# A retention and FFN sandwich on one core: one more tile of x1n by way of VectorE and DRAM, input combinations on VectorE, and a new order at the seam between blocks

## The chip, the cores and the metric

The kernel runs on one core of one Trainium2 chip. The metric is the device time of one execution in microseconds (us), the median of several executions. All engine times below come from one profiled execution.

## The reference

The input x has 4 sequences of 1024 tokens with 512 features, all in f32. With LN a layernorm without weights:

```python
x = x + LN(attn(LN(x)));   x = x + LN(ffn(LN(x)))

attn(x):  q, v, g = x @ Wq.T, x @ Wv.T, silu(x @ Wg.T)       # 512 x 512 each
          ret[t] = lam[head] * ret[t-1] + v[t]                # a scan along the sequence
          return (LN(q * ret) * gamma + beta) * g @ Wo.T
ffn(x):   gate, up = silu(x @ f8(gate_w) * gate_s), x @ f8(up_w) * up_s    # 512 -> 1536
          return gate * up @ f8(down_w) * down_s                           # 1536 -> 512
```

f8() rounds a weight to 8-bit float.

## The kernel before

The 4096 tokens are cut into 8 **blocks** of 512 tokens, each of 4 **tiles** of 128 tokens (s = 0 to 3). The main loop (line 1048) goes over stages t = 0 to 7. Stage t computes the FFN of block t (object `f`), and between its matmuls it slips in the attention of block t+1 (object `b`) and the preparation of block t+2 (object `n`). Inside a stage, i = 0 to 11 goes over the 12 groups of 128 hidden features of the FFN. Every engine works through its instructions in the order in which this loop issues them (`InOrder`, line 66): there is no scheduler that reorders. All instructions have line 74 in the profile, so they are told apart by the names of tiles.

**The FFN of one i.** TensorE multiplies into two PSUM tiles, `pfg` (gate) and `pfu` (up), 8 matmuls each: 4 chunks of features, each with an upper and a lower half of the f32 value of x1n. ScalarE applies silu to `pfg`; VectorE multiplies it with `pfu` (the line `gate<-pfu`); ScalarE casts the product to the upper half `fuse` (`fuse`), and VectorE computes the lower half (`rest`, the line `fuse<-gate,fuse`). Two iterations later TensorE multiplies that by the down weights into `pd`, 8 matmuls. `pfg` and `pfu` take turns in two PSUM buffers (tag `pf`).

**The attention in products.** From block 2 on (`FAST`), each of the four 512x512 projections is computed as 7 products of halves, with sums and differences of halves of the weights and of the data, instead of 8 products. One product is 4 f32 matmuls of 256 columns, recorded as 8. The products are numbered j = 1 to 7 and are made in the order of the list `order` (line 333); `product` (line 481) makes the next one, asks SP for the weights of a later one (`fetch_weights`, a ring of 4 buffers) and lets VectorE or ScalarE take the result out of PSUM. Written v1, v2 and so on for the projection v, what comes after a product is:

- v1: ScalarE copies it to SBUF. v2 adds to the same bank, and VectorE then runs two scans on it.
- v6: in the other bank; VectorE adds the copy of v1 (`mids<-pv`). v7 adds to that bank, again with one VectorE addition; v4, v5 and v3 follow.

The right side of v1 and v2 is a half of the normalized and transposed input `xnT`. The others need a combination of halves in `t_sums`, made by `input_sums` (line 465): combination 1 and then 2 (which reads 1) for v6, 3 for v7, 4 (which reads 2) for v4. One combination is one 128x512 subtraction.

**The seam between stages.** The FFN of block t+1 can start its first `pfg` when x1n of that block is there, transposed and in two halves (`x1nT`), for all four tiles. Per tile the steps are these:

- `o_moments(s)`: mean and variance of the attention's output on VectorE (`st<-mids`, `mv<-st`), and its power -1/2 on GpSimd. The `mv` tiles have 3 buffers.
- `x1_of(s)`: ScalarE normalizes it, GpSimd adds it to x, and SP stores the sum x1 to DRAM (`kept`).
- `x1_moments(s)`, `x1n_of(s)`: the same moments for x1, and VectorE normalizes it (`x1n<-x,mv`).
- The transposition. Tiles 0 and 1 go by `move_x1n` (line 754): VectorE transposes blocks of 32x32 (`xs<-x1n`), SP stores them to DRAM in four pieces (`mxs<-xs`), and a load brings them back in order (`x1n<-mxs`). Tiles 2 and 3 go by `turn_x1n` (line 751): 4 transposes on TensorE into a `pf` tile (`pt`).
- `upper_of(s)`: ScalarE casts the upper half into `x1nT`; `rest_of(s)`: VectorE computes the lower half.

In stages 1 to 5 the instructions of TensorE at the seam are: pfg and pfu of i = 11, v1, pd of i = 9, the transposes of tiles 2 and 3, v2, v6, then pfg of the next stage's i = 0, v7, pfu, v4 and so on. GpSimd makes combinations 1 and 2 at i = 9 and 3 and 4 at i = 11. On VectorE the moments of the output tiles 2 and 3 follow the normalization of tiles 0 and 1; `rest(10)` is issued after `x1n_of(3)` in i = 11; the four `rest_of` come before the scans of v2. Stage 6 has the same seam without `n`: no products and no combinations, with tiles 2 and 3 on TensorE before the change and after it.

Of the kernel before, what the change touches and what calls it, by code (L numbers as in the profile page):

```python
# [23 lines left out]
def retention_ffn_sandwich(  # L24
# [26 lines left out]
    NB = NT // TB  # L51
# [14 lines left out]
    class InOrder:  # L66
# [9 lines left out]
    pe, dve, act, pool, sp = (  # L76
        InOrder(e) for e in (nc.tensor, nc.vector, nc.scalar, nc.gpsimd, nc.sync)
    )
# [138 lines left out]
    def rounds(n, now=True):  # L217
        for _ in range(n):
            next(rounding, None)
            if now:  # L220
                units()
# [75 lines left out]
    def ps_tile(name, home="pa"):  # L297
        if home == "pa":
            pa_turn[0] = 1 - pa_turn[0]
            home = f"pa{pa_turn[0]}"  # L300
        elif home[:2] == "pa":
            pa_turn[0] = int(home[2])
        return homes[home].tile([P, TB], F32, tag=home, name=name)
# [26 lines left out]

    FAST = 2
    H = TB // 2
    order = [("v", j) for j in (1, 2, 6, 7, 4, 5, 3)]
    order += [("q", j) for j in (1, 6, 2, 7, 4, 5, 3)]
    order += [("g", j) for j in (1, 2, 6, 7, 4, 5, 3)]
    order += [("o", j) for j in (1, 2, 6, 5, 3, 7, 4)]
    banks = {
        "v": {1: 0, 6: 1, 5: 0}, "q": {1: 1, 6: 0, 5: 1},
        "g": {1: 0, 6: 0, 5: 1}, "o": {1: 0, 6: 1, 5: 0},
# [38 lines left out]
            sp.dma_start(operands[k][j], t)  # L378

    RING = 4  # L380
    total_products = len(order) * (NB - FAST)
    fetched = [0]

    def fetch_weights():
        n = fetched[0]
        if n < total_products:
            k, j = order[n % len(order)]
            sp.dma_start(w_ring[:, n % RING], operands[k][j])
            fetched[0] += 1

    class Retention:
# [88 lines left out]

        def product(self):

            k, j = order[self.made]
            n = (self.t - FAST) * len(order) + self.made
            self.made += 1
            w = w_ring[:, n % RING]
            if j in (1, 6, 5):
                bank = ps_tile(f"p{k}{j}_{self.t}", f"pa{banks[k][j]}").rearrange("p (c f) -> p c f", c=2)
                if j == 6:
                    self.bank_b = bank  # L490
                else:
                    self.bank_a = bank
            bank = self.bank_b if j in (6, 7, 4) else self.bank_a
            for o in range(2):
                out_ = bank[:, o]
                if k != "o" and len(self.right[j].shape) == 4:
                    out_ = out_.rearrange("p (g j) -> p g j", j=Q)
                for c in range(2):
                    if k == "o":
                        left, right = self.left[j][:, c, ts(o, P)], w[:, c, :]  # L500
                    else:
                        left, right = w[:, c, ts(o, P)], self.right[j][:, c]
                    pe.matmul(
                        out_, left, right,
                        start=(j in (1, 6, 5) and o == 0 and c == 0), stop=True,
                        skip_group_check=True,
                    )
            fetch_weights()
            if k == "o":
                return self.add_o(j, bank)  # L510
            c12, p1, s167 = (mids[:, m] for m in (1, 2, 3))
            if k == "v" and self.t == FAST:

                if j == 1:
                    self.p1 = work.tile([P, 2, H], F32, tag="rstd", name="p1", bufs=1)
                p1 = self.p1
            if j == 1:
                act.copy(p1, bank)
            elif j == 6:
                dve.tensor_tensor(c12, bank, p1, ALU.add)  # L520
            elif j == 7:
                dve.tensor_tensor(s167, bank, p1, ALU.add)
            elif j == 2:
                self.take(k, 0, 0, bank)
            elif j == 4:
                dve.tensor_tensor(p1, bank, p1, ALU.add)
                self.take(k, 1, 0, p1)
            elif j == 5:
                dve.tensor_tensor(s167, bank, s167, ALU.add)
                self.take(k, 1, 1, s167)  # L530
            else:
                dve.tensor_tensor(c12, bank, c12, ALU.add)
                self.take(k, 0, 1, c12)
# [195 lines left out]
        def x1_of(self, s):  # L729
            self.x1n[s] = work.tile([P, D], F32, tag="tok", name=f"x1n_{self.t}_{s}", bufs=4)  # L730
            center = shift_scale if self.fast else self.center
            center(self.x1n[s], self.po.pop(s), self.mvo[s])
            pool.tensor_tensor(self.xt[s], self.xt[s], self.x1n[s], ALU.add)
            self.kept[s] = dram.tile([P, D], F32, tag="kept", name=f"kept_{self.t}_{s}")
            sp.dma_start(self.kept[s], self.xt[s])

# [178 lines left out]
    a = Retention(0, x_first)  # L915
# [20 lines left out]
    b = Retention(1)  # L936
# [63 lines left out]
    a.o_moments(0)  # L1000
    rounds(1)
    a.x1_of(0)
    a.o(1, "pd1")
    a.o_moments(1)
    a.x1_moments(0)
    a.x1_of(1)
    a.x1n_of(0)
    a.o(2, "pd2")
    a.o_moments(2)
    a.x1_moments(1)  # L1010
    a.x1_of(2)
    a.x1n_of(1)
    a.o(3, "pd3")
    a.new_x1nT()
# [2 lines left out]
    a.o_moments(3)  # L1017
    a.x1_moments(2)
    a.x1_of(3)
    a.x1n_of(2)  # L1020
    a.rest_of(0)
    b.q(0, "pf")
# [25 lines left out]
    for t in range(NB):  # L1048
        f, n = Ffn(a), None
        fast = b is not None and b.fast  # L1050
        for i in range(NI):
            if t > 0 and (t > 1 or i) and not (fast and i == 11):
                (f if i else l).rest((i - 1) % NI)
            if t == 0 and i == 0:
                n = Retention(2)
# [36 lines left out]
            for _ in range(look[i][0] if t == 1 else 0):  # L1092
                next(search)

            if fast and i < 10:
                b.product()
            if t == 2 and i == 0:
                next(passing)
# [44 lines left out]
            if fast and i == 7:  # L1143
                b.y_sums(3, 4)
            if fast and i == 9:
                b.x1_moments(0)
                b.x1_moments(1)
            if fast and i == 10:
                b.x1_of(2)
                b.x1_of(3)  # L1150
            units()
            f.up(i)
            if n and i == 11:
# [3 lines left out]
            if t == 0 and i == 10:  # L1157
                load = b.move_x1n(2)
# [2 lines left out]
                load()  # L1161
                keep_sums("g")
                b.o_moments(3)
            if b and i == 11:
                b.x1n_of(3, center_scale)
            if fast and i == 11:
                f.rest(10)
            if n and i == 11:
                n.input_sums(*((3, 4) if fast else (1, 2)))
            if t == 0 and i == 11:  # L1170
                b.upper_of(2)
            if fast and i == 9:
                loads = []
                for s in range(2):
                    b.x1n_of(s)
                    loads.append(b.move_x1n(s))
                for load in loads:
                    load()
                if n:
                    n.input_sums(1, 2)  # L1180
            if fast and i == 11:
                for s in range(2):
                    b.upper_of(s)
                    b.rest_of(s)
# [32 lines left out]
            if fast and i == 8:  # L1217
# [1 line left out]
                b.o_moments(1)  # L1219
                b.x1_of(0)  # L1220
                b.x1_of(1)
            if fast and i == 9:
                b.o_moments(2)
                b.o_moments(3)
            if fast and i == 10:
                b.x1_moments(2)
                b.x1_moments(3)
                b.x1n_of(2)
            if t == 0:
                if i == 3:  # L1230
                    rounds(2, now=False)
                    b.halves()
                    units()
                    rounds(1, now=False)
                elif i < 8:
                    rounds(3, now=False)
                if i == 2:
                    b.halves()
                if i < 11:
                    f.rest(i)  # L1240
                if i < 2:
                    n.stats(i)
# [7 lines left out]
                n.new_xnT()  # L1250
            if b and not fast and 7 <= i <= 10:
                b.x1_of(i - 7)
            if b and not fast and i >= 9:
                b.rest_of(i - 9)
            if n and t > 0 and i in (6, 7):
# [32 lines left out]
            if n and i == 11:  # L1288
                if t == 0:
                    n.product()  # L1290
                else:
                    b.turn_x1n(2, "pf")
                    b.upper_of(2)
                    b.rest_of(2)
                b.turn_x1n(3, "pf")
                b.upper_of(3)
                b.rest_of(3)
                if t == 0:
                    n.input_sums(3, engine=dve)
            if fast and (i < 3 or i in (7, 8)):  # L1300
                b.product()
            if fast and i == 2:
# [6 lines left out]
                b.var()  # L1309
                b.rstd_y()  # L1310
            if n and i == 11:
                n.products(2 if t else 1)
                if t == 0:
                    n.input_sums(4, engine=dve)
                    f.rest(11)
# [9 lines left out]
            if b and i == 4 and 0 < t < NB - 2:  # L1325
                n = Retention(t + 2)
# [4 lines left out]
        l, a, b = f, b, n  # L1331
# [68 lines left out]
```

## Time and profile before

| what | value |
|---|---|
| time, median of 3 runs (lowest, highest) | 971.76 us (971.65, 972.81) |
| time of the profiled execution | 971.97 us |
| its span, first to last instruction | 970.2 us |
| granted clock of TensorE, mean | 0.997 |
| busy: PE, weight loads (PEld), VectorE (DVE), ScalarE (ACT), GpSimd (POOL) | 955.9, 764.3, 678.5, 405.9, 282.8 us |
| first weight load of the transposes at the seams after stages 1 to 6 | 310.45, 427.14, 543.50, 659.72, 775.90, 891.47 us |

PE is TensorE's matmuls and PEld its weight loads; a matmul and its weight load are one step of the same queue. A timeline's row gives the start, the time until the end of the group, the engine, the operation with its output and inputs, and the number of instructions put together; what stands in brackets is the time in which the engine was idle before it, and what ended that. A new instruction can start a little before the one before it has ended, so the spacing of starts is often some 0.08 us shorter than a duration.

### The profile page before, as it was taken

How to read it: one execution, taken by the hardware profiler on the slowest of the kernel's cores; microseconds unless marked ns; L12 is line 12 of the kernel's file. 1: busy time of each engine (PE TensorE's matmuls, PEld its weight loads, DVE VectorE, ACT ScalarE, POOL GpSimd, SP SyncE). 2: the span in 40 equal slices, each digit the busy share in tenths (PEclk: the TensorE clock that was granted, in tenths of full speed). 3: DMA queues.
4: the chain of work that ended last, by engine and by line, in shares of the span. 5: the costliest groups of instructions: out<-in, count | busy, mean ns of one | idle time of the engine just before them, and what ended most of it. 6: DMA issues, size and time to landing. Idle time of an engine off the chain costs nothing.

```text
span 970.2 us, 11799 instructions
## 1 busy us (share of the span) xinstructions
PE 955.9 (99%) x4118; PEld 764.3 (79%) x4118; DVE 678.5 (70%) x1038; ACT 405.9 (42%) x637; POOL 282.8 (29%) x356
## 2 busy tenths in 40 slices
PE   9999999999999999999999999999999999999996
PEld 7455766778888888888888888888888888888885
DVE  5996999676767578586685766767667676657535
ACT  3555674468655135331433315342162421524223
POOL 1404131412327042250523315242142602314020
PEclk9999999999999999999999999999999999999998
DMA  9311423762436426463336524364242632314021
GB/s 297 127 48 61 152 66 97 226 209 87 141 98 181 123 89 215 131 183 100 96 111 177 159 76 133 97 175 140 81 153 92 179 116 85 100 44 131 0 87 44
DMA packets 96060, 119.04 MB, mean 123 GB/s; under 512 B 8320, under 2 KB 58240, under 8 KB 96000
## 3 DMA queue, kind: packets, MB, share of 16 engines
q1 hardware_dynamic: 95136, 117.62, 40.0%
q8 instruction: 33, 0.54, 0.2%
q10 hardware_dynamic: 864, 0.66, 0.2%
q14 instruction: 27, 0.22, 0.1%
HBM read 86.00 MB, written 32.24 MB: 122 GB/s over the span
## 4 chain that ended last, share of the span: by engine, by line
PE 86%; DVE 6%; DMA 2%; ACT 2%; POOL 2%; issue 1%; SPq 0%; DVEq 0%; ACTq 0%; POOLq 0%
PE pfg L74 16%; PE pfu L74 16%; PE pd L74 15%; PE pq L74 10%; PE pv L74 10%; PE pg L74 9%; PE po L74 8%; DVE scr L74 1%; DVE st L74 1%; DVE y L74 1%; POOL mv L74 1%; PE pt L74 1%; ACT x1n L74 1%; DMA wv_sb<-in_wvT 1%; DMA xnT<-mx 1%
## 5 line engine op out<-in xcount | busy, mean ns | idle before, releaser
L74 PE MATMUL pfu<-x1nT,up_sb 128*128 128x512 f32 x768 | 205.0, 409 | 0.0
L74 PE MATMUL pfg<-x1nT,gate_sb 128*128 128x512 f32 x768 | 198.1, 400 | 0.1
L74 PE MATMUL pd<-down_sb,fuse 128*128 128x512 f32 x720 | 189.3, 404 | 0.0
L74 PEld LDWEIGHTS pfu<-x1nT,up_sb 128*128 128x128 f32 x768 | 144.4, 188 | 32.2 <-issue 3.1
L74 PEld LDWEIGHTS pfg<-x1nT,gate_sb 128*128 128x128 f32 x768 | 144.1, 188 | 30.5 <-DVE x1nT L74 0.9
L74 PEld LDWEIGHTS pd<-down_sb,fuse 128*128 128x128 f32 x720 | 135.3, 188 | 27.4
L74 ACT ACTIVATE gate<-pfg,gs_sb 128x512 f32<-128x512 f32 x96 | 65.5, 682 | 169.1 <-PE pfg L74 168.9
L74 ACT CAST fuse<-gate 128x512 fp32r<-128x512 f32 x90 | 55.6, 618 | 176.5 <-DVE gate L74 176.3
L74 DVE SCALAR_TENSOR_TENSOR gate<-pfu,us_sb,gate 128x512 f32<-128x512 f32 x96 | 71.7, 747 | 57.8 <-PE pfu L74 56.5
L74 POOL TENSOR_SCALAR mv<-mv 128x1 f32<-128x1 f32 (+1 forms) x82 | 23.5, 286 | 263.3 <-DVE mv L74 260.1
L74 DVE TENSOR_TENSOR fuse<-gate,fuse 128x512 fp32r<-128x512 f32 x90 | 76.8, 853 | 5.5 <-ACT fuse L74 5.5
L74 POOL TENSOR_TENSOR ysum<-y 128x256 f32<-128x256 f32 (+1 forms) x14 | 14.3, 1023 | 196.7 <-DVE y L74 196.7
L74 DVE BATCH_NORM_STATS2 st<-x 128x6 f32<-128x512 f32 x64 | 43.6, 681 | 28.9 <-POOL x L74 26.2
L74 POOL TENSOR_TENSOR mv<-mv,nhalf 128x1 f32<-128x1 f32 (+1 forms) x75 | 48.6, 648 | 6.2
L74 PE MATMUL pv<-t_sums,w_ring 128*128 128x256 f32 x192 | 45.6, 380 | 0.5 <-POOL t_sums L74 0.5
L74 PE MATMUL pg<-t_sums,w_ring 128*128 128x256 f32 x192 | 45.7, 380 | 0.0
L74 PE MATMUL po<-w_ring,t_sums 128*128 128x256 f32 x192 | 45.4, 379 | 0.0
L74 PE MATMUL pq<-t_sums,w_ring 128*128 128x256 f32 x192 | 45.3, 379 | 0.0
L74 POOL TENSOR_TENSOR x<-x,x1n 128x512 f32<-128x512 f32 x32 | 41.5, 1295 | 13.2 <-ACT x1n L74 12.8
L74 PEld LDWEIGHTS pv<-t_sums,w_ring 128*128 128x128 f32 x192 | 36.1, 189 | 6.8 <-issue 0.8
L74 PEld LDWEIGHTS pg<-t_sums,w_ring 128*128 128x128 f32 x192 | 35.9, 189 | 6.5 <-ACT mids L74 1.3
L74 PEld LDWEIGHTS po<-w_ring,t_sums 128*128 128x128 f32 x192 | 36.2, 189 | 6.0 <-issue 0.5
(168 smaller groups left out, 1512.9 us busy)
## 6 DMA issues: line engine op xcount, KB each, us to landing
kept<-x SPq DMA_DIRECT2D x32, 256.0 KB, 2.8
x<-kept SPq DMA_DIRECT2D x32, 256.0 KB, 4.0
x<-in_x SPq DMA_DIRECT2D x28, 256.0 KB, 4.2
out<-d SPq DMA_DIRECT2D x27, 256.0 KB, 2.1
xnT<-mx SPq DMA_DIRECT2D x24, 256.0 KB, 5.0
w_ring<-dsum_v SPq DMA_DIRECT2D x24, 256.0 KB, 2.9
w_ring<-dsum_q SPq DMA_DIRECT2D x24, 256.0 KB, 2.6
w_ring<-dsum_g SPq DMA_DIRECT2D x24, 256.0 KB, 2.7
```

The costliest lines, as they stand in the source:

```text
L74: return lambda *args, **kwargs: tc.keep_in_program_order(op(*args, **kwargs))
```

## The change

There are four edits, all in stages 1 to 6 (stage 0 and the tail issue the same instructions as before).

1. In stages 1 to 5 tile 2 of x1n goes by `move_x1n`; only tile 3 goes by TensorE. Its load is issued at i = 11.
2. In the same stages the four combinations of a block's halves are made on VectorE: 1 and 2 at i = 10, 3 and 4 at the seam.
3. The order at the seam: v6 comes before v2 for blocks 3 and up, and a fourth product (v7) is made ahead of the next stage's first `pfg`, which then has one product fewer in i = 0. VectorE's `rest_of` and combinations are spread between these products.
4. In stages 1 to 6, at i = 9, the moments of the output tiles 2 and 3 and their `x1_of` come ahead of the normalization of tiles 0 and 1, `x1n_of(3)` moves to i = 10, and `rest(10)` is issued at the start of i = 11. The stores to `kept` are issued by a function of their own.

```diff
+    for t in range(FAST, NB):
+        order += [("v", j) for j in ((1, 2, 6, 7, 4, 5, 3) if t == FAST else (1, 6, 2, 7, 4, 5, 3))]
...
-            if t > 0 and (t > 1 or i) and not (fast and i == 11):
+            if t > 0 and (t > 1 or i):
                 (f if i else l).rest((i - 1) % NI)
...
-            if fast and i < 10:
+            if fast and i < 10 and (i or b.t == FAST):
                 b.product()
...
             if fast and i == 9:
-                b.x1_moments(0)
-                b.x1_moments(1)
-            if fast and i == 10:
-                b.x1_of(2)
-                b.x1_of(3)
+                b.o_moments(2)
+                b.o_moments(3)
             units()
             f.up(i)
...
             if fast and i == 9:
+                b.x1_moments(0)
+                b.x1_moments(1)
+                b.x1_of(2)
+                b.x1_of(3)
                 loads = []
                 for s in range(2):
                     b.x1n_of(s)
                     loads.append(b.move_x1n(s))
+                b.keep_x1(2)
+                b.keep_x1(3)
                 for load in loads:
                     load()
-                if n:
-                    n.input_sums(1, 2)
+            if n and fast and i == 11:
+                load()
...
-            if fast and i == 9:
-                b.o_moments(2)
-                b.o_moments(3)
             if fast and i == 10:
                 b.x1_moments(2)
                 b.x1_moments(3)
                 b.x1n_of(2)
+                b.x1n_of(3)
+                if n:
+                    load = b.move_x1n(2)
+                    n.input_sums(1, 2, engine=dve)
...
             if n and i == 11:
                 if t == 0:
                     n.product()
...
                 else:
-                    b.turn_x1n(2, "pf")
-                    b.upper_of(2)
-                    b.rest_of(2)
-                b.turn_x1n(3, "pf")
-                b.upper_of(3)
-                b.rest_of(3)
+                    n.product()
+                    b.turn_x1n(3, "pf")
+                    for s in range(2):
+                        b.upper_of(s)
+                        b.rest_of(s)
+                    n.input_sums(3, engine=dve)
+                    n.product()
+                    for s in (3, 2):
+                        b.upper_of(s)
+                        b.rest_of(s)
+                    n.input_sums(4, engine=dve)
...
             if n and i == 11:
-                n.products(2 if t else 1)
+                n.product()
```

More of the change, by code (lines that the diff above doesn't have):

```diff
@@ L332, in retention_ffn_sandwich @@
     H = TB // 2
[L333 to L336, printed above, removed]
+    order = []
+    for t in range(FAST, NB):
+        order += [("v", j) for j in ((1, 2, 6, 7, 4, 5, 3) if t == FAST else (1, 6, 2, 7, 4, 5, 3))]
+        order += [("q", j) for j in (1, 6, 2, 7, 4, 5, 3)]
+        order += [("g", j) for j in (1, 2, 6, 7, 4, 5, 3)]
+        order += [("o", j) for j in (1, 2, 6, 5, 3, 7, 4)]
     banks = {
@@ L380, in retention_ffn_sandwich @@
     RING = 4
-    total_products = len(order) * (NB - FAST)
+    total_products = len(order)
     fetched = [0]
@@ L386, in fetch_weights @@
         if n < total_products:
-            k, j = order[n % len(order)]
+            k, j = order[n]
             sp.dma_start(w_ring[:, n % RING], operands[k][j])
@@ L481, in product @@
         def product(self):
-            k, j = order[self.made]
-            n = (self.t - FAST) * len(order) + self.made
+            n = (self.t - FAST) * (len(order) // (NB - FAST)) + self.made
+            k, j = order[n]
             self.made += 1
@@ L733, in x1_of, with keep_x1 @@
             pool.tensor_tensor(self.xt[s], self.xt[s], self.x1n[s], ALU.add)
+        def keep_x1(self, s):
             self.kept[s] = dram.tile([P, D], F32, tag="kept", name=f"kept_{self.t}_{s}")
@@ L1002, in retention_ffn_sandwich @@
     a.x1_of(0)
+    a.keep_x1(0)
     a.o(1, "pd1")
@@ L1006, in retention_ffn_sandwich @@
     a.x1_of(1)
+    a.keep_x1(1)
     a.x1n_of(0)
@@ L1011, in retention_ffn_sandwich @@
     a.x1_of(2)
+    a.keep_x1(2)
     a.x1n_of(1)
@@ L1019, in retention_ffn_sandwich @@
     a.x1_of(3)
+    a.keep_x1(3)
     a.x1n_of(2)
@@ L1163, in retention_ffn_sandwich @@
                 b.o_moments(3)
-            if b and i == 11:
+            if t == 0 and i == 11:
                 b.x1n_of(3, center_scale)
[L1166 to L1169, printed above, removed]
+            if t == 0 and i == 11:
+                n.input_sums(1, 2)
             if t == 0 and i == 11:
@@ L1176, in retention_ffn_sandwich @@
                     loads.append(b.move_x1n(s))
+                b.keep_x1(2)
+                b.keep_x1(3)
                 for load in loads:
                     load()
-                if n:
-                    n.input_sums(1, 2)
-            if fast and i == 11:
+            if n and fast and i == 11:
+                load()
+            if fast and i == 11 and not n:
                 for s in range(2):
@@ L1221, in retention_ffn_sandwich @@
                 b.x1_of(1)
-            if fast and i == 9:
-                b.o_moments(2)
-                b.o_moments(3)
+                b.keep_x1(0)
+                b.keep_x1(1)
             if fast and i == 10:
@@ L1252, in retention_ffn_sandwich @@
                 b.x1_of(i - 7)
+                b.keep_x1(i - 7)
             if b and not fast and i >= 9:
@@ L1290, in retention_ffn_sandwich @@
                     n.product()
-                else:
-                    b.turn_x1n(2, "pf")
-                    b.upper_of(2)
-                    b.rest_of(2)
-                b.turn_x1n(3, "pf")
-                b.upper_of(3)
-                b.rest_of(3)
-                if t == 0:
-                    n.input_sums(3, engine=dve)
+                    b.turn_x1n(3, "pf")
+                    b.upper_of(3)
+                    b.rest_of(3)
+                    n.input_sums(3, engine=dve)
+                else:
+                    n.product()
+                    b.turn_x1n(3, "pf")
+                    for s in range(2):
+                        b.upper_of(s)
+                        b.rest_of(s)
+                    n.input_sums(3, engine=dve)
+                    n.product()
[3 more added lines that the diff above has]
+                    n.input_sums(4, engine=dve)
             if fast and (i < 3 or i in (7, 8)):
```

## The prediction

> **What bounds the kernel now.** The page's first part comes first: the share of each engine.
>
> ```profile
> PE 955.9 (99%) x4118; PEld 764.3 (79%) x4118; DVE 678.5 (70%) x1038; ACT 405.9 (42%) x637; POOL 282.8 (29%) x356
> ```
>
> TensorE is never without a started matmul for long, so time is won only by fewer steps in its queue and lost by every wait in it. The step that the change takes out is at the seams. I take the one after stage 3, in the timeline of weight loads:
>
> ```profile
> 538.13 1.77 PEld L74 LDWEIGHTS pfu<-x1nT,up_sb 128*128 128x128 f32 x8
> 539.94 1.71 PEld L74 LDWEIGHTS pv<-xnT,w_ring 128*128 128x128 f32 x8
> 541.68 1.78 PEld L74 LDWEIGHTS pd<-down_sb,fuse 128*128 128x128 f32 x8
> 543.50 1.02 PEld L74 LDWEIGHTS pt<-ident,x1n 128*128 128x128 f32 x8
> 544.49 1.60 PEld L74 LDWEIGHTS pv<-xnT,w_ring 128*128 128x128 f32 x8
> 546.11 1.70 PEld L74 LDWEIGHTS pv<-t_sums,w_ring 128*128 128x128 f32 x8
> 547.84 1.78 PEld L74 LDWEIGHTS pfg<-x1nT,gate_sb 128*128 128x128 f32 x8
> 549.66 1.71 PEld L74 LDWEIGHTS pv<-t_sums,w_ring 128*128 128x128 f32 x8
> ```
>
> No row has an idle time in brackets: pfu, v1, pd, both transposes, v2, v6, pfg, v7 follow one another. A product takes 1.73 of the queue, an FFN group 1.82. What VectorE does meanwhile shows why nothing waits:
>
> ```profile
> 542.00 1.51 DVE L74 TENSOR_SCALAR x1n<-x,mv 128x512 f32<-128x512 f32 x1
> 543.43 1.77 DVE L74 TENSOR_TENSOR fuse<-gate,fuse 128x512 fp32r<-128x512 f32 x1
> 545.12 1.28 DVE L74 TENSOR_TENSOR x1nT<-x1n,x1nT 128x512 fp32r<-128x512 f32 x2
> 546.33 1.28 DVE L74 TENSOR_TENSOR x1nT<-pt,x1nT 128x512 fp32r<-128x512 f32 x2
> 547.53 1.37 DVE L74 TENSOR_TENSOR_SCAN y<-lam,carry,pv 128x256 f32<-128x256 f32 x2
> 548.82 0.66 DVE L74 TENSOR_TENSOR mids<-pv,mids 128x512 f32<-128x512 f32 x1
> 549.40 0.68 DVE L74 TENSOR_TENSOR fuse<-gate,fuse 128x512 fp32r<-128x512 f32 x1
> ```
>
> The four lower halves (`x1nT`) end at 547.61, before pfg needs them at 548.06; the scans come behind. From start to start a lower half costs 0.60, the two scans 1.29, an addition 0.58 to 0.61. The first two rows are stretched (0.55 and 0.67 elsewhere) while GpSimd makes combinations 3 and 4.
>
> Two seams do wait. After stage 5:
>
> ```profile
> 765.77 1.30 POOL L74 TENSOR_TENSOR t_sums<-xnT 128x512 f32<-128x512 f32 x1 [2.18 <-DMA xnT<-mx]
> 772.28 0.69 DVE L74 BATCH_NORM_STATS2 st<-x 128x6 f32<-128x512 f32 x1 [3.97 <-POOL x L74]
> 777.45 0.42 PEld L74 LDWEIGHTS pt<-ident,x1n 128*128 128x128 f32 x4 [0.96 <-DVE x1n L74]
> ```
>
> GpSimd waits for the input's load with the powers of tiles 2 and 3 queued behind; that delays x1, its moments, and at last the transpose of tile 3. After stage 6:
>
> ```profile
> 890.15 0.75 DVE L74 SCALAR_TENSOR_TENSOR gate<-pfu,us_sb,gate 128x512 f32<-128x512 f32 x1
> 894.65 1.45 PEld L74 LDWEIGHTS pfg<-x1nT,gate_sb 128*128 128x128 f32 x7 [0.29 <-DVE x1nT L74]
> ```
>
> Here the lower halves already end the wait, and they hang on `gate` of i = 11 by way of ScalarE's casts.
>
> **Transposes out.** Eight of them take 0.99, and the product behind them 1.62 in place of 1.73, so tile 2's four cost 0.44. Five seams: -2.2.
>
> The Trainium skill (VectorE: DVE Perf Modes, Rules for kernel authors) speaks against this edit: for a 128x128 transpose it names TensorE where PSUM may be the destination, and its section on the three transpose paths gives 390 ns for one in bf16. By that figure, as an estimate, four would cost 1.56 and the five seams save 7.8; the sum below would then end near 971. The row of this trace decides here, and it is 0.44 for four.
>
> **Combinations off GpSimd.** The wait after stage 5 goes, as GpSimd's powers have nothing ahead of them. From pd to pfu that seam takes 10.96 (774.08 to 785.04), the one after stage 3 9.71 (541.68 to 551.39): -1.25. Nothing else of GpSimd's was late.
>
> **VectorE up to the seam.** Counted forward in stage 3: o4 is taken at 527.66 as before, moments of output tiles 2 and 3 to 529.9, `gate` of i = 9 to 530.6. The moments of x1's tile 1 want the `mv` buffer that ScalarE's `x1_of(2)` still reads, until some 532.7; then x1n_0 and its transpose, x1n_1 (1.5, as in the first VectorE row above, since GpSimd now adds x there) and its transpose to 536.3, the lower half of i = 9, `gate` of i = 10 at 537.1 to 537.9. Moments of x1's tiles 2 and 3 to 539.4; each power takes 0.9, so x1n_2 starts at 539.6, x1n_3 at 540.4, the transpose of tile 2 at 540.9, combinations 1 and 2 end at 542.9, `gate` of i = 11 runs at 543.5. pfu of i = 11 wants its buffer at 538.13 and v6 its combination at 543.50: covered by 0.25 and 0.55. I put both at nothing; with the cover gone, every us is a us of TensorE, at most 0.5 per seam.
>
> **The wait at v7.** TensorE's queue is now pfu, v1, pd, v6, transposes of tile 3, v2, v7, pfg. v6 starts at 543.50 in place of the transposes. VectorE takes a product 2.14 after its first load (549.66 to 551.80 for v7 before), so at 545.65. Behind that stand two lower halves, 0.61 + 2 x 0.60, then combination 3 from 547.46. On VectorE a combination takes 0.68 (the seam after stage 0 has two there), so it ends at 548.14. v7 reads it, and would be reached at 543.50 + 1.73 + 0.50 + 1.62 = 547.35; with 0.06 from VectorE's end to the load (198.88 to 198.94 at the seam after stage 0) it starts at 548.20. That is a wait of 0.85, five times: +4.25. Bounds: 0.4 (spacings a sixth shorter) and 1.3 (lower halves at their mean of 0.75 in the groups, with a stretched neighbour).
>
> **The wait at pfg.** Behind combination 3 VectorE has the scans of v2 (548.06 to 549.35, v2 done at 547.8), then the lower halves of tiles 3 and 2, ending at 550.62. pfg's first load is at 548.20 + 1.73 = 549.93; the second multiplies by a lower half and would come at 550.15, and comes at 550.68: 0.53, five times +2.65. Before, the scans stood behind these halves; that is what turns here. Tile 2's trip must be over, too: transpose done at 541.6, four stores some 0.5 apart, the last issued by 543.4, landing 2.1 later, SP's load then 2.8, in ScalarE's upper half by 549 to 549.9. I put it at nothing; landings of up to 3.9 would make it 0.9 per seam. On SP the stores and that load stand ahead of the weights of v4, v5 and v3, wanted from 554 on; `kept` of tiles 2 and 3 now stand ahead of the loads of tiles 0 and 1, wanted at 544.8 and back by 543.5. No cost.
>
> **After stage 6.** x1n_3 and the lower half of i = 10 now stand ahead of `gate` of i = 11. By the same forward count (349.71 later than stage 3) x1n_3 ends at 890.7, that half at 891.3, and `gate` starts at 891.2 in place of 890.15; the cast, the upper and lower halves follow, all 1.05 later: +1.0 (0 if x1n_3 is quicker than counted, 1.2 at most).
>
> **Sum.** -2.2 - 1.25 + 4.25 + 2.65 + 1.0 = +4.45 on the profiled execution's 971.97: 976.4. That execution lies 0.21 above the median, so 976.2.
>
> **Rivals.**
>
> Quicker: VectorE is freed of the stretched rows (1.0 each, twice per seam), the combinations are there in time, and no wait forms: -2.2 - 1.25, or 968.3. This decides from the point where combination 3 ends by 547.3, so that VectorE does four operations in 1.7 after v6. They add up to 2.49, and none is stretched in that sum. Chance 0.08.
>
> Even: the waits are half as long, as VectorE's queue has slack I have not seen, and stage 6 keeps its order of events: 3.45 against 3.45, 971.8. For it speaks that every step of VectorE up to the seam was counted, not shown. Chance 0.12.
>
> Late trip: besides the waits forecast, tile 2 lands 0.9 too late and v6 or pfu waits 0.5: 5 x 1.4 = 7 more, 983. For it speaks the small cover. Chance 0.10.
>
> **How the numbers follow.** The forecast has 0.70. Its own range, with 0.7 to 2.1 per seam for both waits and 0 to 1.2 for stage 6, is 5 x (0.26 to 1.66) - 1.25 + (0 to 1.2): 972.0 to 980.2. A measurement here can tell 0.2%, or 1.9 us: faster is below 969.8, slower above 973.7. Of the forecast 0.03 lies below 973.7, so slower 0.67 + 0.10, same 0.12 + 0.03, faster 0.08. The range goes from within the even case to within the late trip, 970.5 to 982.
>
> **What would show it.** Right: a bracket before the second `pv<-t_sums` of the seams after stages 1 to 5, naming VectorE's `t_sums`, of some 0.85, and one in pfg named `x1nT`, of some 0.5; four transposes in 0.5; no wait before `pt` after stage 5; 1.3 in place of 0.29 after stage 6. Wrong: no bracket at v7; or brackets at v6, pfu or pfg that name `xs`, `x1n` or a DMA, which would say that the chain up to the seam or the trip is the late one.

## The result, and the profile after

| | before | changed |
|---|---|---|
| time, median of 4 runs of each (lowest, highest) | 971.7 us (971.38, 972.81) | 978.45 us (977.53, 978.81) |
| ratio, 95% interval | | 1.0067 (1.0055 to 1.0078) |
| profiled execution, its span | 971.97, 970.2 us | 977.53, 975.5 us |

The forecast was 976.2 with a range of 970.5 to 982; slower had 0.77. The changed kernel is slower by 0.67%, and the interval excludes 1. Its profiled execution is its fastest one, 0.9 below the median.

Where the time went can be read from the starts of the same weight loads in both profiles. The table gives how much later than before the loads behind each seam start, less how much later those ahead of it did; "rest" is what came up before the first of these seams and inside the stages. The first six columns and "rest" of the changed kernel add up to 5.00; another 0.32 comes up behind the last loads that were compared, and 0.24 outside the span.

| seam after stage | 1 | 2 | 3 | 4 | 5 | 6 | rest |
|---|---|---|---|---|---|---|---|
| changed, measured | 1.03 | 0.75 | 1.14 | 0.73 | -0.40 | 1.64 | 0.11 |
| forecast | 0.94 | 0.94 | 0.94 | 0.94 | -0.31 | 1.0 | 0 |

The page's share of the engines first (busy time, share, instructions), to be held against the first line of the prediction: TensorE lost 20 loads, four per seam, VectorE gained 25 instructions and GpSimd lost 20.

```profile
PE 957.0 (98%) x4098; PEld 762.3 (78%) x4098; DVE 689.1 (71%) x1063; ACT 405.9 (42%) x637; POOL 254.5 (26%) x336
```

In the list of waits (engine, what it was about to do, what it waited for: total, times, longest) these three are new or larger:

```profile
PEld pv L74 <- DVE t_sums L74: 4.5, 5, 0.9
PEld pfg L74 <- DVE x1nT L74: 4.3, 7, 0.9
PEld pfg L74 <- ACT x1nT L74: 1.4, 2, 1.1
```

The first is the wait at v7, at five seams of five. A fourth, 0.50 before `over_all`, comes once, at the seam after stage 1 (see e4). The seam after stage 3 in the timeline of weight loads, v2, v7 and the two parts of pfg:

```profile
547.74 1.60 PEld L74 LDWEIGHTS pv<-xnT,w_ring 128*128 128x128 f32 x8
550.23 1.59 PEld L74 LDWEIGHTS pv<-t_sums,w_ring 128*128 128x128 f32 x8 [0.89 <-DVE t_sums L74]
552.16 0.19 PEld L74 LDWEIGHTS pfg<-x1nT,gate_sb 128*128 128x128 f32 x1 [0.34 <-ACT x1nT L74]
552.89 1.48 PEld L74 LDWEIGHTS pfg<-x1nT,gate_sb 128*128 128x128 f32 x7 [0.54 <-DVE x1nT L74]
```

VectorE in the same stretch (the bracket of the first row names ScalarE, but this addition starts 2.22 after the first load of v6, as it does after stage 1, where its bracket names v6):

```profile
547.69 0.69 DVE L74 TENSOR_TENSOR mids<-pv,mids 128x512 f32<-128x512 f32 x1 [1.18 <-ACT x1nT L74]
548.29 1.28 DVE L74 TENSOR_TENSOR x1nT<-x1n,x1nT 128x512 fp32r<-128x512 f32 x2
549.50 0.68 DVE L74 TENSOR_TENSOR t_sums<-xnT 128x512 f32<-128x512 f32 x1
550.10 1.38 DVE L74 TENSOR_TENSOR_SCAN y<-lam,carry,pv 128x256 f32<-128x256 f32 x2
551.39 0.66 DVE L74 TENSOR_TENSOR x1nT<-pt,x1nT 128x512 fp32r<-128x512 f32 x1
552.15 0.69 DVE L74 TENSOR_TENSOR x1nT<-x1n,x1nT 128x512 fp32r<-128x512 f32 x1
```

After v6's addition come two lower halves, then combination 3, which ends at 550.18, and v7 starts at 550.23. After the two scans come the lower halves of tiles 3 and 2, and pfg's second load starts 0.05 after the last one ends. Tile 2 has its x1n back from its trip (the way through DRAM) just then: ScalarE's cast of it runs from 551.50 to 552.12, after 2.81 of waiting for the load, and the last lower half starts at 552.15. So two chains end within 0.1 of one another ahead of pfg, VectorE's queue and tile 2's trip; the wait names only the one that came last.

The wait of tile 3's transposes after stage 5 is gone; the row has no bracket:

```profile
781.44 0.58 PEld L74 LDWEIGHTS pt<-ident,x1n 128*128 128x128 f32 x4
```

After stage 6, VectorE's `gate` of i = 11 and then the two parts of pfg, which waited 1.95 together where it was 0.29 before:

```profile
895.18 0.74 DVE L74 SCALAR_TENSOR_TENSOR gate<-pfu,us_sb,gate 128x512 f32<-128x512 f32 x1
...
898.63 0.19 PEld L74 LDWEIGHTS pfg<-x1nT,gate_sb 128*128 128x128 f32 x1 [1.10 <-ACT x1nT L74]
899.67 1.46 PEld L74 LDWEIGHTS pfg<-x1nT,gate_sb 128*128 128x128 f32 x7 [0.85 <-DVE x1nT L74]
```

### The profile page after: what moved, and what is told of

Its sections match the earlier page's. It is cut to its first block, busy times and chain, and to the rows that moved or that the text cites. A ratio compares the mean times of both kernels' runs of the same rounds, so it can differ in the third digit from the quotient of the medians.

```text
span 975.5 us, 11801 instructions
## 1 busy us (share of the span) xinstructions
PE 957.0 (98%) x4098; PEld 762.3 (78%) x4098; DVE 689.1 (71%) x1063; ACT 405.9 (42%) x637; POOL 254.5 (26%) x336
## 4 chain that ended last, share of the span: by engine, by line
PE 73%; DVE 14%; DMA 4%; ACT 4%; issue 2%; POOL 2%; SPq 0%; DVEq 0%; ACTq 0%; POOLq 0%
PE pfg L74 14%; PE pfu L74 13%; PE pd L74 12%; PE pq L74 10%; PE pg L74 9%; PE po L74 8%; PE pv L74 6%; DMA kept<-x 2%; DVE st L74 2%; DVE gate L74 2%; DVE fuse L74 2%; DVE x1nT L74 2%; ACT x1n L74 1%; DVE y L74 1%; DVE xs L74 1%
## 5 line engine op out<-in xcount | busy, mean ns | idle before, releaser
L74 DVE TENSOR_TENSOR fuse<-gate,fuse 128x512 fp32r<-128x512 f32 x90 | 73.5, 817 | 5.5 <-ACT fuse L74 5.5
```

Source lines behind the costliest of these rows:

```text
L74: return lambda *args, **kwargs: tc.keep_in_program_order(op(*args, **kwargs))
```

## The experiments

The theory: TensorE's queue at the seams is as short as forecast, and what it waits for is VectorE's order. The rivals were that the waits are independent of one another, that tile 2's trip sets them, or, after stage 6, that something other than `gate` does. All ratios are to the kernel before, measured again beside each run (971.8 to 972.2). The changed kernel was not. The intervals of e1 to e5, e8 and e12, all within 1.4 of its 978.45, overlap its own, so what tells them from it is the profile and not the time.

| run | what | median us | ratio (95%) |
|---|---|---|---|
| e1 | stage 6: `gate` of i = 11 first | 978.86 | 1.0067 (1.0053, 1.0081) |
| e2 | combination 3 early | 977.56 | 1.0059 (1.0046, 1.0071) |
| e3 | scans late | 977.97 | 1.0059 (1.0047, 1.0072) |
| e4 | e2 and e3 together | 977.29 | 1.0053 (1.0040, 1.0066) |
| e5 | stage 6 in the order of before | 977.11 | 1.0051 (1.0038, 1.0064) |
| e6 | e4, e5 and an earlier trip | 972.27 | 1.0002 (0.9993, 1.0011) |
| e7 | before, combinations 1 and 2 of stage 5 on VectorE | 971.52 | 0.9995 (0.9986, 1.0004) |
| e8 | tile 2 back on TensorE | 977.64 | 1.0057 (1.0043, 1.0071) |
| e9 | e6 and `total` early | 970.21 | 0.9984 (0.9975, 0.9992) |
| e10 | e9, stores on two queues | 970.39 | 0.9982 (0.9973, 0.9991) |
| e11 | e9 with tile 2 on TensorE | 970.68 | 0.9988 (0.9979, 0.9997) |
| e12 | combinations back on GpSimd | 979.27 | 1.0072 (1.0060, 1.0085) |

And what the seams gained or lost against the profile of before, read as in the table above:

| run | 1 | 2 | 3 | 4 | 5 | 6 | rest |
|---|---|---|---|---|---|---|---|
| e4 | 1.50 | 0.96 | 0.21 | 0.04 | -0.88 | 1.65 | 1.42 |
| e6 | 1.07 | -0.39 | 0.33 | -0.43 | -1.64 | -0.01 | 0.72 |
| e9 | -0.58 | -0.01 | 0.20 | -0.41 | -1.70 | 0.38 | 1.04 |
| e10 | -0.58 | -0.43 | -0.22 | -0.36 | -1.70 | 0.37 | 0.87 |
| e11 | -0.15 | 0.03 | 0.05 | 0.02 | -1.23 | 0.02 | -0.17 |

**e2: combination 3 early.**

```diff
                     b.turn_x1n(3, "pf")
+                    n.input_sums(3, engine=dve)
                     for s in range(2):
                         b.upper_of(s)
                         b.rest_of(s)
-                    n.input_sums(3, engine=dve)
```

> Changed kernel, with combination 3 issued ahead of the lower halves of tiles 0 and 1 on VectorE, all else as it is. Theory (the waits at v7 and pfg are two readings of one VectorE queue that ends with the lower half of tile 2): the wait before v7 goes (0 in place of 0.89), the wait in pfg grows from about 0.55 to about 1.4, and the time stays at 978.4 (within 1 us). Rival (the two waits are independent, each worth what it shows): v7's wait goes, pfg's stays at 0.55, five seams save 4.4, time 974.0.

v7 waits at no seam, and the time is 977.56. The wait moved to pfg. After stage 5, where it was 0.67:

```profile
785.76 0.19 PEld L74 LDWEIGHTS pfg<-x1nT,gate_sb 128*128 128x128 f32 x1 [0.37 <-ACT x1nT L74]
787.04 1.46 PEld L74 LDWEIGHTS pfg<-x1nT,gate_sb 128*128 128x128 f32 x7 [1.09 <-DVE x1nT L74]
```

The rival falls: 4.5 of waits removed gave at most 0.9, and in the profile the five seams lost 3.3, as in the changed kernel. The two brackets of a seam are one lateness, paid in two places.

**e3: scans late.**

```diff
-                    n.product()
                     for s in (3, 2):
                         b.upper_of(s)
                         b.rest_of(s)
+                    n.product()
```

> Changed kernel, with the lower halves of tiles 3 and 2 issued on VectorE ahead of v2's two scans, as before the change, combination 3 where the change has it. Theory: the wait before v7 stays at 0.85 to 0.9 (same queue ahead of it); the wait in pfg goes, because 1.29 of scans no longer stands ahead of the lower halves; five seams save 0.55 each, 978.45 - 2.7 = 975.7. Rival (tile 2's trip through DRAM is as late as the scans): pfg still waits 0.3 to 0.5, now for ScalarE's upper half, and the time is 977 to 978.4.

The time is the rival's, 977.97. With the scans out of the way, pfg waits for tile 2's trip at the seams after stages 2 and 3; ScalarE's cast waited 3.26 for the load after stage 3. At the other three the wait of pfg goes or falls to 0.33, as the theory had it, but after stage 1 `over_all` then waits 1.44 (see e4). After stage 3:

```profile
553.33 0.19 PEld L74 LDWEIGHTS pfg<-x1nT,gate_sb 128*128 128x128 f32 x1 [0.79 <-ACT x1nT L74]
554.05 1.48 PEld L74 LDWEIGHTS pfg<-x1nT,gate_sb 128*128 128x128 f32 x7 [0.54 <-DVE x1nT L74]
```

The second wait is what remains after a late cast: the lower half behind it.

**e4: both.** The edits of e2 and e3 together.

> Changed kernel with both orders: combination 3 ahead of the lower halves of tiles 0 and 1, and the lower halves of tiles 3 and 2 ahead of v2's scans. Theory (the loss is the order on VectorE and nothing else at the seams): both waits go, 5 x 0.89 + 5 x 0.55 = 7.2 less, 978.45 - 7.2 = 971.3, the time before the change; what is saved by the transposes and by the combinations is then eaten by stage 6 alone. Rival (tile 2's trip ends at the same time as the scans): pfg waits 0.3 to 1.0 per seam for ScalarE's upper half, 973 to 976.

977.29: worse than either said. v7 waits nowhere, and pfg waits at every seam, 0.54 to 1.58, for the trip and the lower half behind it. Seams 3 to 5 gain 0.5 to 0.9 against the changed kernel, seam 1 loses 0.5, seam 2 0.2, and "rest" 1.3, much of it in two waits before a `po` (1.01 and 0.60; see the last section). At seam 1, a row that the prediction had not looked at became the end of the chain, the product `over_all` of stage 2, made once, ahead of the first pfu:

```profile
320.41 0.30 PEld L74 LDWEIGHTS over_all<-total,mean_r 128*128 128x128 f32 x2 [1.78 <-issue]
```

The changed kernel has this wait already, shorter and under another name:

```profile
319.54 0.30 PEld L74 LDWEIGHTS over_all<-total,mean_r 128*128 128x128 f32 x2 [0.50 <-PE pfg L74]
```

In both, and in e3 and e6, `over_all` starts 0.11 to 0.12 after VectorE has ended the sum `total` that it reads (in the changed kernel the sum ends at 319.42).

**e8: tile 2 back on TensorE.**

```diff
+                    b.turn_x1n(2, "pf")
                     b.turn_x1n(3, "pf")
```

and `move_x1n(2)` with its load taken out.

> Changed kernel, with tile 2 back on TensorE's transposes (edit 1 undone, no trip of tile 2), all else as changed. Theory (VectorE's queue from v6 to the lower half of tile 2 sets pfg; the transposes only fill a wait): v7's wait is 0.45 instead of 0.89 as TensorE comes 0.44 later, pfg's is about the same 0.55, the time 978.0 to 978.6. Rival 1 (the saved transposes are a gain of their own): 978.4 + 2.2 = 980.6. Rival 2 (tile 2's trip sets pfg, not VectorE's queue): pfg's waits go, 976.

977.64, the theory's side, and rival 1 is out: the 20 transposes came back and cost nothing in the time (in the profile the five seams lost 3.6 where it was 3.25, not 2.2 more), for TensorE waits at v7 by just so much less.

```profile
550.71 1.59 PEld L74 LDWEIGHTS pv<-t_sums,w_ring 128*128 128x128 f32 x8 [0.46 <-DVE t_sums L74]
```

Rival 2 falls too: the trip alone is not what sets pfg in the changed kernel. Taking away either chain leaves the other.

**e12: combinations back on GpSimd.**

```diff
-                    n.input_sums(1, 2, engine=dve)
+                    n.input_sums(1, 2)
...
-                    n.input_sums(3, engine=dve)
+                    n.input_sums(3)
...
-                    n.input_sums(4, engine=dve)
+                    n.input_sums(4)
```

> Changed kernel, with combinations 1 to 4 of stages 1 to 5 back on GpSimd (edit 2 undone), in the places where the change has them. Theory (combination 2 would end some 1.2 after v6 is reached, as GpSimd takes 1.30 for one and starts them behind the powers): v6 waits about 1.2, v7's wait goes, pfg waits about 0.75; some 0.5 more per seam, 981. Rival (GpSimd has the combinations ready, and VectorE's queue is shorter by one at the seam): no wait at v6, 975.

979.27, but this median is not of the edit alone. In the profile TensorE stood idle for 1.76 ahead of pfg after stage 2, and from 437.3 to 440.7 its granted clock was 0.5, so that seam lost 3.75, some 1.7 of it, half of that stretch, by the slower clock. Three of the five executions have a mean clock of 0.995 or 0.996; the two with 0.998 took 977.87 and 977.99, no more than the changed kernel. Whether the wait brought the clock down, no run shows. Neither sum was right (981 and 975). v6 waits at most 0.03: `pd` ahead of it ended as combination 2 did (548.18). v7 does not wait either. But pfg does, 1.15 to 2.71 per seam, for tile 2's trip and the lower half behind it, and the rows of stage 3 show why it is late: x1n_3, which stands ahead of tile 2's 32x32 transpose, runs beside GpSimd's combination 1 and takes 1.48, where it took 0.55 in the changed kernel.

```profile
545.54 1.48 DVE L74 TENSOR_SCALAR x1n<-x,mv 128x512 f32<-128x512 f32 x1 [0.44 <-POOL mv L74]
```

```profile
545.48 1.26 POOL L74 TENSOR_TENSOR t_sums<-xnT 128x512 f32<-128x512 f32 x1
```

**e1: stage 6, `gate` first.**

```diff
-            if t > 0 and (t > 1 or i):
+            if t > 0 and (t > 1 or i) and not (fast and not n and i == 11):
                 (f if i else l).rest((i - 1) % NI)
...
+            if fast and not n and i == 11:
+                b.x1n_of(3)
+                f.rest(10)
...
-                b.x1n_of(3)
                 if n:
+                    b.x1n_of(3)
```

> Changed kernel, but in stage 6 alone x1n_3 and the lower half of i = 10 are issued on VectorE behind the gate of i = 11 instead of ahead of it. Theory (the loss after stage 6 comes from that gate's delay): the gate of i = 11 starts some 1.0 to 1.5 us earlier within its stage, the two pfg waits after stage 6 shrink from 1.10 + 0.85 to about 0.3 to 0.5 together, and the time falls by 1.5 us from 978.45 to about 977.0. Rival (the loss comes from the order of the tiles 2 and 3 in stage 6, not from the gate): the waits stay at 1.5 to 2.0 together and the time stays at 978.4.

978.86: no gain in the time, and in the profile the seam after stage 6 lost 1.31 in place of 1.64, so the theory falls. `gate` of i = 11 did start 1.6 earlier in its stage (2.28 after the first load of pfu of i = 11, against 3.87). But ScalarE's casts, which had come behind it without a wait, now wait for tiles 0 and 1 to come back from DRAM:

```profile
897.28 0.62 ACT L74 CAST x1nT<-x1n 128x512 fp32r<-128x512 f32 x1 [0.48 <-DMA x1n<-mxs]
898.55 0.62 ACT L74 CAST x1nT<-x1n 128x512 fp32r<-128x512 f32 x1 [0.65 <-DMA x1n<-mxs]
```

VectorE's transpose of tile 0 starts 4.61 ahead of pfu of i = 11 here and in the changed kernel, and 6.94 ahead in the kernel before: the fourth edit, output tiles 2 and 3 first, delays tiles 0 and 1 by 2.3.

**e5: stage 6 in the order of before.** As e1, and in stage 6 `o_moments`, `x1_of` of tiles 2 and 3 come behind `x1n_of` of tiles 0 and 1 again:

```diff
             if fast and i == 9:
-                b.o_moments(2)
-                b.o_moments(3)
+                if n:
+                    b.o_moments(2)
+                    b.o_moments(3)
+                else:
+                    b.x1_moments(0)
+                    b.x1_moments(1)
...
+            if fast and not n and i == 9:
+                b.o_moments(2)
+                b.o_moments(3)
```

> Changed kernel, with stage 6 alone back in the order of before (moments of x1's tiles 0 and 1 and their trips ahead of the moments of output tiles 2 and 3; x1n_3 and the lower half of i = 10 behind the gate of i = 11). Theory (in stage 6 the new order delays two chains by about as much, the gate of i = 11 and the trips of tiles 0 and 1, which is why advancing the gate alone gave nothing): both come back, the wait in pfg after stage 6 falls from 1.10 + 0.85 to about 0.3, and the time falls by 1.6, to 976.8. Rival (what is late after stage 6 hangs on the seams before it): the waits stay near 1.9 and the time at 978.4.

977.11, 1.34 below the changed kernel. The intervals of the two ratios overlap, so it is the profile that shows the gain; the seam's loss is 0.11 in place of 1.64:

```profile
898.80 1.46 PEld L74 LDWEIGHTS pfg<-x1nT,gate_sb 128*128 128x128 f32 x7 [0.41 <-DVE x1nT L74]
```

No run puts the trips of tiles 0 and 1 back and leaves `gate` late. That `gate` alone would hold the seam up, too, is read from the changed kernel's profile, where the casts stand behind it without a wait for the trips.

**e6: all orders.** e4 and e5, and

```diff
                 if n:
-                    b.x1n_of(3)
                     load = b.move_x1n(2)
+                    b.x1n_of(3)
```

> Changed kernel with combination 3 and the lower halves of tiles 3 and 2 early, as in the run with both orders, stage 6 as before the change, and tile 2's 32x32 transpose on VectorE ahead of x1n_3, which starts tile 2's trip through DRAM some 0.9 earlier. Theory (with the VectorE order mended, tile 2's trip is what pfg waits for, 0.54 to 1.58 per seam): pfg's waits shrink by up to 0.9 each, together some 3.5, and stage 6 gives 1.6: 977.3 - 5.1 = 972.2. Rival (the trip ends where SP's queue and the landings put it, not where it starts): the waits at the seams stay, only stage 6 gives: 975.7.

972.27 against 972.2 expected, which is luck in part: 2.7 of it lies outside the span in the median, where the kernel before has 1.8 and the changed one 2.0, and no trace shows why. By the median span it is 969.5, against 970.4 for the kernel before beside it. The five seams together lose 2.9 less than in e4, stage 6 loses 1.66 less. The trip was the end of the chain in e4; started earlier, it ends earlier. What is left is `over_all` at seam 1 (1.78 again), where VectorE has this behind the seam's work and a `fuse`:

```profile
319.47 0.18 DVE L74 TENSOR_REDUCE total<-over 128x1 f32<-128x24 f32 x1
```

**e9: `total` early.**

```diff
             for _ in range(look[i][0] if t == 1 else 0):
                 next(search)
+            if t == 1 and i == 11:
+                next(passing)
...
-            if t == 2 and i == 0:
-                next(passing)
```

> The run with all orders mended, and beside that the sum `total`, which TensorE's `over_all` product of stage 2 reads, is made on VectorE one step earlier, in i = 11 of stage 1 and not in i = 0 of stage 2. Theory (the 1.78 left at the seam after stage 1 is TensorE waiting for `total`, which stands behind the seam's lower halves, scans, combination 4 and `fuse` on VectorE): the 1.78 goes, that seam ends 0.44 earlier than before the change instead of 1.07 later, time 972.27 - 1.5 = 970.8. Rival (the row is a gap of TensorE's own, as its releaser is given as issue): nothing changes, 972.3.

970.21. Seam 1 ends 0.58 earlier than before the change, and `over_all` has no bracket:

```profile
317.95 0.42 PEld L74 LDWEIGHTS over_all<-total,mean_r 128*128 128x128 f32 x2
```

So "issue" in that row stood for a wait on VectorE. This version is faster than the kernel before by 0.16% (0.9984, interval below 1). Its profiled execution is its slowest, 1.2 above the median.

**e10: two queues.** For the trip of tile 2 alone (`by_act`):

```diff
-            sp.dma_start(
+            (act if b >= NQ // 2 and by_act else sp).dma_start(
                 m[:, b].rearrange("(a i) c j -> i a (c j)", a=NQ),
```

> The same with two of tile 2's four stores issued by ScalarE instead of SP. Theory (the trip is the four issues of 0.44 one after the other, one landing and one load; halving the issues starts the load 0.9 earlier): the waits of pfg that are left at the seams (0.87 at one seam in the run with all orders mended) go, 970.8 - 0.5 = 970.3. Rival (the landings decide, or ScalarE's casts come later by the issues): 970.8 or up to 1 more.

970.39, no difference that can be told from e9. The issues do run side by side, two in 0.79 and two in 0.84 where four took 1.79 (the timelines of SP and of ScalarE, stage 3):

```profile
541.11 0.79 SPq L74 DMA_DIRECT2D mxs<-xs  x2
```

```profile
541.11 0.84 ACTq L74 DMA_DIRECT2D mxs<-xs  x2
```

Counted from the start of tile 2's transpose, in stage 3 of the two profiles, its load is issued 4.16 later instead of 5.01, but the cast that needs it starts 7.79 later instead of 8.22: half of the gain is lost between the load's issue, a row of 0.86 in place of 0.34, and its landing. The Trainium skill (DMA: Bandwidth & Descriptors, Rules for kernel authors) says of spreading transfers over SP and ACT that it saves issue time alone; these rows agree.

**e11: the mended order with tile 2 on TensorE.** e9 without the load of tile 2, and with

```diff
-                    load = b.move_x1n(2)
                     b.x1n_of(3)
...
+                    b.turn_x1n(2, "pf")
                     b.turn_x1n(3, "pf")
```

> The run with all orders mended and `total` early, with tile 2 back on TensorE's transposes (no trip of tile 2). Theory (once no wait is left behind them, the 0.44 of four transposes count at every seam): 970.8 + 2.2 = 973.0. Rival (the transposes still stand in a wait, as where they were put back without the orders): no change, 970.8.

970.68: 0.47 above e9, where the theory had 2.2 more and the rival nothing, and its interval overlaps that of e9. In the profile the 0.44 is there where nothing else is late: seams 1, 4 and 5 are 0.43 to 0.47 better with the trip (e9) than with TensorE (e11), seams 2 and 3 are not (0.04 better, 0.15 worse), since pfg waits there for the trip. So four transposes cost about the 0.44 of the prediction, and not the 1.56 of its estimate. The rest of e9's seam gain goes in the stages and after stage 6 (1.04 and 0.38), where e11 has none; but the profile of e9 is of its slowest execution, and that of e11 is at its median. The page's rule cited in the prediction, TensorE for such a transpose, is thus neither confirmed nor refuted by the time.

**e7: the kernel before, one stage mended.**

```diff
-                    n.input_sums(1, 2)
+                    n.input_sums(1, 2, engine=dve if t == 5 else pool)
```

> The kernel before, with combinations 1 and 2 on VectorE instead of GpSimd in stage 5 alone; nothing else of the change. Theory (the one real gain of the second edit is that GpSimd's powers no longer stand behind combinations that wait for the input's load): the 0.96 before the transposes after stage 5 goes, from pd to pfu that seam takes 9.7 instead of 10.96, time 971.85 - 1.25 = 970.6. Rival (1.4 of VectorE's time ahead of the moments delays the same chain): the wait stays or moves, 971.8 or more.

In the profile the wait goes and seam 5 gains 1.05; all other seams are within 0.03.

```profile
775.49 1.02 PEld L74 LDWEIGHTS pt<-ident,x1n 128*128 128x128 f32 x8
```

The median is 0.63 lower and its interval includes 1, so the time does not show it by itself. e11, which gains 1.23 there and at most 0.15 at any other seam, is faster by 0.12% with an interval below 1.

## Why the prediction was right, and where it was not

**Right side, size within 2.3 us.** The five seams were put at 5 x 0.94 - 1.25 = 3.45 and came to 3.25; stage 6 was put at 1.0 and came to 1.64. The sum fell 1.1 short of the profiled execution (0.64 at stage 6, 0.2 the other way at the five seams, 0.1 in "rest", and 0.6 that no term stood for, at the end and outside the span) and 2.3 short of the median. The 0.9 between the profiled execution and the median is not explained by a trace.

That the five seams came out within 0.2 is luck in part. The waits were longer than forecast: 4.45 for 4.25 at v7, 3.3 for 2.65 at pfg, and 0.50 at `over_all`. Against that, the loads behind a wait go by quicker, some 0.1 each time (v7's row takes 1.59 here and 1.71 before), twice at each seam. The prediction counted that behind the transposes alone.

**v7: right.** 0.89 for 0.85, at all five seams, by the chain as counted: with v6 at 545.47 instead of 543.50 the forecast start of 548.20 becomes 550.17, and v7 started at 550.23.

**pfg: right in size, half right in cause.** 0.54 to 0.67 for 0.53 by VectorE, and 0.34 more at one seam by the trip. The prediction put tile 2's trip at nothing; it ended level with VectorE's queue, and it is what e3 and e4 ran into.

**The covers of v6 and of pfu of i = 11: right to within 0.1.** No bracket at either. But pfu starts 1.86 to 1.92 behind the first load of pfg at all six seams, where 1.81 to 1.82 is the spacing before: its cover was used up.

**The wait after stage 5: right,** gone (-0.40 there against 0.73 to 1.14 at the others). e7 and e11 measured 1.05 and 1.23 for 1.25.

**The terms are not additive: missed.** The sum was right because all of them were true at once, but a reader who takes them one by one is misled: the transposes' -2.2 with its four loads per seam is no gain while TensorE waits behind them (e8), and neither wait could be had back alone (e2, e3). The waits that the changed kernel has at its seams and the kernel before has not come to 9.9 (8.3 at the five seams, 1.66 after stage 6). Only with all the chains moved (e6) did the time fall by most of that, 6.2 from 978.45, with 2.65 of waits left at seams 1 and 3.

**Stage 6: the term that was mis-sized.** The step is "all 1.05 later: +1.0", by x1n_3 and a lower half ahead of `gate`. x1n_3 itself waited for GpSimd's powers (0.25 and 0.44 before the last two x1n), so `gate` came 1.56 later against pfu of i = 11 (3.87 for 2.31), and the term was 1.64. The named cause was also only one of two: e1 took it away and gained 0.33 at the seam and nothing in the time, because the trips of tiles 0 and 1 start 2.3 later by the fourth edit; e5 took both away.

**`over_all`: not in the sum.** At the seam after stage 1 the queue of VectorE goes on to `total`. In the changed kernel it waited 0.50 there, behind the seam's own waits (seam 1 lost 1.03 where seams 2 and 4 lost 0.75 and 0.73), and 1.78 once these were mended.

**The rivals.** Quicker needed combination 3 by 547.3 in the time of before; it ended at 548.21 (550.18 less 1.97). Even fell with it. Late trip came at one seam in the profile, by 0.34 and not at v6 or pfu, but at pfg.

## What to carry to other kernels

Where an in-order engine waits twice within a few us for another in-order engine, ask whether it is one lateness paid in two places: then neither wait is worth its own length, and moving one operation up only moves the bracket. Before taking a wait away, find the chain that ends next behind it; here it stood less than 0.1 behind (the trip) or was hidden altogether (tiles 0 and 1, `total`), and each had to be moved before the time fell. Work taken out of a queue is worth its length only at places where the queue is not waiting.

## What had not been expected of the hardware

- The end of the trip through DRAM varies: within the profiled execution of the changed kernel the stores `mxs<-xs` landed 1.6 to 3.3 after their issue (median 1.8), the loads back 2.5 to 4.0 (median 2.9). As an estimate from these spreads, a chain with a store and a load needs 1.1 to 2.6 of cover beyond the medians, not the 0.1 it had.
- A wait named "issue" was VectorE's `total` once (1.78, gone in e9). Between the seams another stands before a product `po` of stages 2 and 3, 0.26 to 1.01 in the changed kernel and most versions of it (in e9 0.70 and 0.83; in the kernel before once, 0.30). It ends with VectorE too: wherever it stands, the load starts 0.06 to 0.08 after VectorE's addition `mids<-po` has ended. In stage 2 this addition stands behind a transpose of `xn`, that waits for ScalarE, and ScalarE for a store of `xn` to DRAM (`mx<-xn`): 3.76 to 4.40 in the versions whose `po` waits there, 3.19 to 3.60 in those whose does not (the kernel before, e7, e11, e12). In stage 3 that wait for the store is 2.8 to 2.9 in all of them, so there it is something else. No run moved this chain. Its waits are as large as what separates e9, e10 and e11.
